# Layer 0 of a four-layer attention and expert stack: routing of the first half placed beside the attention of the other two batches, a constant score row made once, two products merged, loads reordered

## The chip, the cores and the metric

The kernel runs on one NeuronCore of one Trainium2 chip, as a single launch. A core has five engines that run beside each other and are held together by semaphores: PE (TensorE, matrix products; its weight loads are listed apart as PEld), DVE (VectorE), ACT (ScalarE), POOL (GpSimd) and SP (SyncE, which here only issues DMAs and loads registers). Sixteen DMA engines move data between the device memory and the on-chip memory. The metric is the device time of one execution in microseconds (us). Three runs of the kernel before took 1406.45, 1413.10 and 1416.71 us; the median is 1413.1 us.

## What is computed

The input `x` has 4 batches of 512 tokens with 128 features, in float32; `ctx_1024` has 154 rows of 128 features for each batch. Four layers follow each other, and each adds a cross attention and then a mixture of 8 experts to `x`, both of the normalised `x`. This case touches layer 0 alone. Its attention is this (`x` normalised is `encoder_hc`, the context is `decoder_hq`):

```python
w1, w2, w3 = (w_sim[:d], w_sim[d:2 * d], w_sim[2 * d:])
Sim = (encoder_hc @ w1)[:, :, None] + (decoder_hq @ w2)[:, None, :] \
    + jnp.einsum('bid,bjd->bij', encoder_hc * w3, decoder_hq) + b_sim[0]
A = jax.nn.softmax(Sim, axis=2)
hq_hat = jnp.einsum('bij,bjd->bid', A, decoder_hq)
Batt = jax.nn.softmax(jnp.max(Sim, axis=2), axis=1)
hc_bar = jnp.einsum('bi,bid->bd', Batt, encoder_hc)[:, None, :]
hc_hat = jnp.broadcast_to(hc_bar, encoder_hc.shape)
feats = jnp.concatenate([encoder_hc, hq_hat, encoder_hc * hq_hat, encoder_hc * hc_hat], axis=-1)
hcq = feats @ W_qv + b_qv
```

The term `decoder_hq @ w2` is the same for all tokens of a batch. The term `encoder_hc * hc_hat` multiplies each feature by one number of the batch. The expert part of layer 0 takes, for each token, the two experts with the largest of 8 gate values and adds their outputs with softmax weights:

```python
gate_logits = x @ Wg + bg
top_vals, top_idx = jax.lax.top_k(gate_logits, TOP_K)          # TOP_K = 2
h = jnp.einsum('td,edh->eth', xf, W0) + b0[:, None, :]
g = jax.nn.silu(jnp.einsum('td,edh->eth', xf, W1) + b1[:, None, :])
y = jnp.einsum('eth,ehd->etd', h * g, W2) + b2[:, None, :]
```

## The kernel before

**Tiles.** Batch `b` of `x` stays on chip for the whole kernel as `x[b]`, 128 partitions by 4 row tiles (`NI`) by 128 features. The four batches are handled as two halves: half 0 is batches 0 and 1, half 1 is batches 2 and 3.

**Start (L104 to L226).** SP first loads the four batches (L108), then the context in two pieces, `cm` and `ctail` (L112, L113). DVE and POOL make masks and constants. PE transposes the context (L193, L197), and DVE copies it to `ctxT` and to two other arrangements (L194 to L202). L1218 to L1226 load the gate weights and biases of all four layers in nine small DMAs. `layer0_setup` (L956) then loads the score weights `w_sim`, which PE turns into columns (`columns`, L204), the biases and the four 128x128 output matrices `wqv`, and makes two operands: `rhs1` (L964, the context times w3 plus w1) and `w2b` (L966, the column w2 repeated 128 times). L1322 fills two token buffers in device memory, `buf`, with zeros.

**Attention of a batch.** `prepare(b)` normalises `x[b]` (L240), transposes it to `xnT` (L248), and makes the scores of each row tile with two accumulated products, `xnT` by `rhs1` (L975) and `w2b` by `ctxT` (L976). DVE adds the scalar bias while it moves the scores to `sim` (L979), takes row maxima (L987), and ACT makes exponentials with row sums (L992). `tile_of(b)` scales `sim` (L1000), transposes it (L1004, L1009), and multiplies it with the context (L1012, L1013), which gives `hq`. The softmax over the tokens goes through a maximum over partitions (L1016 to L1025), an exponential (L1027), four products with `xn` (L1030) and four with a matrix of ones, which add the exponentials up (L1032). Out of these come three feature tiles `ft` (L1038 to L1040); four products for each of the four row tiles, one per feature block, sum to the output (L1045), which DVE adds to `x[b]` (L1053, L1054).

**Routing of a half.** `route(layer, half)` (L650) is a generator with a `yield` between its stages: statistics of the two batches, which end in a power on POOL (L233); normalising; transposing; gate products (L665); the two largest of eight (`top`, L625); counts and ranks by triangular products (L692, L694); slot numbers `su` (L716) and the expert of each block, `eb` (L744); softmax weights (L769 to L777); and at its end the contribution of the second bias `b2`, which is added to `x` (L792 to L804). At the slot numbers it queues sixteen scatters for POOL in `rows_due` (L733). Each is an indirect DMA (L721) that sends 128 normalised rows to their slots in `buf[half]`. `row_transfers` (L640) issues what is queued.

**Experts of a half.** `experts(layer, half)` (L824) reads `buf[half]` back in groups of four blocks of 128 tokens (`tok`, L838; the load waits for all sixteen scatters), transposes them (L848), and for each of 23 blocks reads the expert number into a register (L856), loads this expert's weights (`w`, L864, three buffers), and does 8 up products (L875), an activation (L890, L891), 4 down products (L902) and a store (L911). Later POOL gathers the outputs (L935), and they are added to `x` (`combine`, L947).

**Order.** `attend_first` (L1257) is the order of layer 0, as written out by hand:

```python
tiles = prepare(0, found[0])
for b in range(B):
    tiles(0)
    if b == 1:
        found.update({k: stats(x[k]) for k in range(2, B)})
    if b == 2:
        beside = Steps(route(layer, 0, *gates[layer]))
    if b < B - 1:
        tiles = prepare(b + 1, found[b + 1])
    if b == 2:
        beside.step(6)
return beside.finish()
```

So `prepare(b + 1)` follows tile `b`, the routing of half 0 is called after the tile of batch 2, and the scatters are issued by the `row_transfers()` at L1331, after the last tile. Then the experts of half 0 begin (L1334), with the routing of half 1 (L1337) between their blocks, its scatters paced two by two behind the blocks' output copies (L910).

Within layer 0 the instructions aren't bound to this order: a scheduler orders each engine's queue at build time by its own estimate, and the written order is one of its inputs. In layers 1 to 3 the attention's order on PE, ACT and DVE is fixed by hand (L1283). [...] Buffers come from pools by tag: two tiles of one tag share its buffers, and a new tile waits until the old one has been read. The tags that matter here are `rows` (two buffers: `w_sim`'s rows, and for layer 1 the wide copies and `wo_r` at L1076), `wv` (one), `aT` (one), `probs` (two), and in PSUM `sc`, `tr` and `av` (two each).

## Time and profile before

| What | us |
|---|---|
| Median of three runs (lowest, highest) | 1413.1 (1406.45, 1416.71) |
| The profiled execution | 1326.58 |
| Its span, first to last instruction | 1324.7 |
| Outside the span | 1.9 |

The profiled execution is 6.1% shorter than the median of the runs. Sums below are made against its own span, and then set beside the median. It had a mean granted TensorE clock of 0.930 of full speed.

The span divides into stages that can be told by which lines run in them. The columns are the stage, its length, PE's busy time, DVE's busy time, and the granted PE clock.

| Stage (us from the start) | Length | PE busy | DVE busy | PE clock |
|---|---|---|---|---|
| Layer 0: start, attention, routing and scatter of half 0 (0 to 118) | 118 | 74.5 | 60.8 | 0.77 |
| Layer 0: experts (118 to 290) | 172 | 151.9 | 92.2 | 0.96 |
| Layer 1: attention (290 to 480) | 190 | 143.8 | 127.8 | 0.89 |
| Layer 1: experts (480 to 600) | 120 | 102.8 | 57.2 | 0.93 |
| Layer 2: attention (600 to 850) | 250 | 233.6 | 158.2 | 0.99 |
| Layer 2: experts (850 to 930) | 80 | 55.0 | 31.2 | 0.89 |
| Layer 3: attention (930 to 1190) | 260 | 242.1 | 159.7 | 0.97 |
| Layer 3: experts (1190 to 1324) | 134 | 95.6 | 61.3 | 0.91 |

How to read it: an engine's busy time is time with an instruction in execution. Matmuls are pipelined, so overlapping ones aren't counted twice, and a busy PE needn't be at its peak. A line such as `L1045 PE MATMUL av<-wqv,ft` names the line in the kernel, the engine, the operation, and the tiles written and read. In a timeline the first number is the start in us from the start of the span, the second the duration of the group, and what stands in brackets is how long the engine had been idle and what ended that. A float32 product appears as two passes, so `x8` is four products.

### The profile page before, as it was taken

To read this page: it belongs to the slowest core of one execution; us is meant where nothing else is said; L and a number is where in the kernel's file an instruction comes from. 1 tells how busy PE (TensorE), PEld (TensorE's weight loads), DVE (VectorE), ACT (ScalarE), POOL (GpSimd) and SP (SyncE) were. 2 spreads that over 40 slices of the span, in tenths; PEclk is the share of its full clock that TensorE was granted. 3 is DMA by queue.
4 is the path that set the end of the run, shared out by engine and by line. 5 is a ranking of instruction groups with operands and counts; after the bars stand their busy time and mean duration, and the time that the engine had idled before them with its cause. 6 is when DMAs were issued, how large, how long until landed. Compare 5 with 4: busy or idle time off the path is not lost.

```text
span 1324.7 us, 26947 instructions
## 1 busy us (share of the span) xinstructions
PE 1099.2 (83%) x9435; PEld 904.1 (68%) x9435; DVE 748.5 (57%) x2057; ACT 588.2 (44%) x2290; POOL 252.4 (19%) x281
## 2 busy tenths in 40 slices
PE   4885897897777778988999999857899999899881
PEld 3774887773343445877787778746778887789781
DVE  5572554656767566433666766424376676646452
ACT  1112443355444444536556655322565665533230
POOL 2023122204000020221000004045030000403424
PEclk8786998998899889989999999988999999999996
DMA  7013575552101121553112223444421211335762
GB/s 220 0 61 98 163 225 179 171 156 80 26 9 37 38 62 50 151 148 93 42 38 46 49 50 102 127 144 140 132 62 34 50 34 33 83 91 163 202 184 57
DMA packets 136996, 126.82 MB, mean 96 GB/s; under 512 B 13466, under 2 KB 116511, under 8 KB 136479
## 3 DMA queue, kind: packets, MB, share of 16 engines
q1 hardware_dynamic: 129695, 110.39, 30.0%
q0 software_dynamic: 7168, 14.69, 3.8%
q8 instruction: 78, 1.28, 0.4%
q14 instruction: 55, 0.45, 0.1%
HBM read 101.31 MB, written 23.72 MB: 94 GB/s over the span
## 4 chain that ended last, share of the span: by engine, by line
PE 38%; DVE 7%; DMA 6%; ACT 3%; issue 3%; POOL 2%; SPq 1%; POOLq 0%; DVEq 0%; ACTq 0%
PE sc L608 5%; PE sc L875 5%; PE tr L368 5%; PE tr L422 4%; PE av L405 4%; PE av L902 4%; DMA w<-in_up 4%; PE sc L593 2%; PE av L387 2%; ACT probs L305 2%; DVE nm L291 2%; POOL yg L935 1%; PE sc L557 1%; PE tr L848 1%; DVE aT L412 1%
## 5 line engine op out<-in xcount | busy, mean ns | idle before, releaser
L305 ACT ACTIVATE probs<-sc,nm 128x154 f32<-128x154 f32 x768 | 286.3, 402 | 169.1 <-DVE nm L291 169.0
L875 PE MATMUL sc<-tokT,w 128*128 128x128 f32 x1528 | 210.8, 287 | 32.8 <-DMA w<-in_up 26.7
L875 PEld LDWEIGHTS sc<-tokT,w 128*128 128x128 f32 x1528 | 189.7, 198 | 46.6 <-DMA w<-in_up 13.0
L291 DVE TENSOR_REDUCE nm<-sc 128x6 f32<-128x924 f32 x144 | 143.2, 1011 | 86.6 <-PE sc L608 50.7
L902 PE MATMUL av<-w,hT 128*128 x1160 | 173.4, 284 | 10.1 <-DVE hT L891 7.3
L305 ACT ACTIVATION_READ_ACCUMULATOR probs<-sc,nm 128x1 f32 x768 | 168.2, 219 | 0.0
L902 PEld LDWEIGHTS av<-w,hT 128*128 128x128 f32 x1160 | 149.9, 195 | 21.2 <-DVE hT L891 11.4
L935 POOL DMA_INDIRECT yg<-ybuf,su x112 | 106.7, 953 | 275.6 <-DVE pT L261 63.7
L233 POOL TENSOR_TENSOR rstd<-ve,nhalf 128x4 f32<-128x4 f32 x32 | 33.2, 1039 | 619.4 <-DVE ve L231 499.2
L721 POOL DMA_INDIRECT buf<-xn,su x112 | 108.1, 965 | 171.3 <-DVE hT L891 43.7
L261 DVE COPY pT<-tr 128x512 f32<-128x512 f32 x160 | 107.4, 688 | 49.2 <-PE tr L368 43.9
L368 PE MATMUL tr<-ident,probs 128*128 128x128 f32 x768 | 121.5, 289 | 0.8 <-DVE rT L334 0.6
L405 PE MATMUL av<-pT,vm 128*64 128x128 f32 (+1 forms) x1536 | 102.7, 284 | 8.8 <-DVE pT L261 8.7
L890 ACT ACTIVATE eg<-sc,w 128x128 f32<-128x128 f32 x184 | 66.2, 367 | 98.5 <-DVE hT L891 72.7
L368 PEld LDWEIGHTS tr<-ident,probs 128*128 128x128 f32 x768 | 86.0, 145 | 28.8 <-issue 12.7
L891 DVE SCALAR_TENSOR_TENSOR hT<-sc,w,eg 128x128 f32<-128x128 f32 x184 | 63.0, 348 | 55.1 <-ACT eg L890 52.7
L910 DVE COPY ys<-av 128x128 f32<-128x128 f32 x168 | 48.5, 289 | 78.7 <-PE av L902 73.3
L405 PEld LDWEIGHTS av<-pT,vm 128*64 128x64 f32 (+1 forms) x1536 | 65.3, 127 | 35.6 <-issue 18.2
L608 PE MATMUL sc<-kT,qT 64*128 64x154 f32 x1024 | 86.5, 308 | 3.5 <-ACT probs L305 3.5
L608 PEld LDWEIGHTS sc<-kT,qT 64*128 64x128 f32 x1024 | 71.0, 189 | 14.3 <-issue 9.7
L593 PE MATMUL sc<-xnT,wq 128*128 128x128 f32 x512 | 67.1, 286 | 2.9 <-ACT probs L305 2.9
L422 PE MATMUL tr<-wo,aT 128*128 128x128 f32 x512 | 66.1, 284 | 1.6 <-DVE xnT L253 1.3
(252 smaller groups left out, 1477.7 us busy)
## 6 DMA issues: line engine op xcount, KB each, us to landing
w<-in_up SPq DMA_DIRECT2D x46, 516.0 KB
w<-in_up SPq DMA_DIRECT2D x76, 258.0 KB
rep<-rd SPq DMA_DIRECT2D x64, 256.0 KB
ybuf<-ys SPq DMA_DIRECT2D x168, 64.0 KB
tok<-buf SPq DMA_DIRECT2D x36, 256.0 KB
w<-in_down SPq DMA_DIRECT2D x3, 2048.0 KB
w<-in_up SPq DMA_DIRECT2D x46, 128.0 KB
buf<-zero SPq DMA_DIRECT2D x2, 1472.0 KB
```

Of the source, the lines that this page charges most:

```text
L261: return nc.vector.tensor_copy(o, i)
L291: nc.vector.tensor_reduce(self.at.heads(self.nm, g, n), self.sc[g][:, :, 0 : n * S2].rearrange("p j (s k) -> p j s k", s=n), AX.X, ALU.max ...
L305: nc.scalar.activation(self.pr[:, h, :], self.sc[g][:, j, s * S2 : (s + 1) * S2], AF.Exp, bias=self.nm[:, h : h + 1], accum_out=self.rs[:, ...
L368: nc.tensor.transpose(q[:, t * P : (t + 1) * P], self.pr[:, h, 0:P], ident)
L405: nc.tensor.matmul(av[rows, cols], v, self.pT[n][:, t, :], start=False, stop=last)
L422: nc.tensor.matmul(o[:, 0:D], self.aT[:, c, :], self.at.wo[:, c, :], start=(c == 0), stop=(c == self.nb - 1))
L593: nc.tensor.matmul(sc[:, c // 4, c % 4 * P : (c % 4 + 1) * P], wq[:, c * P : (c + 1) * P], at.xnT[:, i * P : (i + 1) * P], start=True, sto ...
L608: nc.tensor.matmul(sc[:, j, s * S2 : (s + 1) * S2], at.qT[i][rows, c, :], at.kT[rows, c, :], start=True, stop=True)
L721: ins = nc.gpsimd.indirect_dma_start(out=buf[half], out_offset=bass.IndirectOffsetOnAxis(ap=su[:, t : t + 1], axis=0), in_=xns[t // NI][:, ...
L875: nc.tensor.matmul(dst, w[:, at : at + P], xT, start=True, stop=True)
L902: nc.tensor.matmul(y[:, 0:D], hT[:, fc, :], w2[:, bass.ds(e, 1), fc, :].rearrange("p o d -> p (o d)"), start=(fc == 0), stop=(fc == nf - 1),)
L935: ins = nc.gpsimd.indirect_dma_start(out=yg[:, t, :], out_offset=None, in_=ybuf[half], in_offset=bass.IndirectOffsetOnAxis(ap=su[:, t : t ...
```

## The change

The change touches the loads at the start, `columns`, `layer0_setup` with `prepare` and `tile_of`, `attend_first`, and where the gates are loaded.

- Loads: the first batch of `x`, then `w_sim`, then the context, then the other three batches. The nine gate loads move from ahead of `layer0_setup` to behind it; the statistics of all four batches are asked for ahead of them.
- The constant score row: `row`, two products of `w2b` with the context of two batches each (4 x 154 columns in all) plus the bias, is made once. The scores then need one product for each row tile, and DVE adds `row` where it added the scalar bias.
- Merged products: the number `hc` of each feature is put into the weights, `wc = wqv[3] * hc + wqv[0]`, and the output needs three products for each row tile in place of four. The sum of the exponentials comes from ACT's accumulator (`accum_out=es`), and one product with ones in place of four.
- Order: `prepare(0)`, `prepare(1)`, tile 0, `prepare(2)`, tile 1, then three steps of the routing of half 0, `prepare(3)`, five further steps (up to the slot numbers), the scatters, tile 2, one step, tile 3, the rest.
- Buffers: `w2b` takes tag `rows` in place of `wv`, where `row` now lies; `sim` takes `probs` (two buffers) in place of `aT` (one); `ft` takes `vm`, and `wc` takes `res1`.

```diff
...
 
 
     x_in = a["x"].rearrange("b (i p) d -> b p i d", p=P)
-    x = []
-    for b in range(B):
-        t = xpool.tile([P, NI, D], F32, tag=f"x{b}", name=f"x{b}")
-        nc.sync.dma_start(t, x_in[b])
-        x.append(t)
+    x = [xpool.tile([P, NI, D], F32, tag=f"x{b}", name=f"x{b}") for b in range(B)]
+    nc.sync.dma_start(x[0], x_in[0])
+    sim_rows = p2.tile([3, P], F32, tag="rows", name="sim_rows")
+    nc.sync.dma_start(sim_rows, a["L0_xattn_w_sim"].rearrange("(k p) -> k p", p=P))
     cmt = w1.tile([P, 2, B, D], F32, tag="wo", name="cmt")
     cm, ctail = cmt[:, 0], cmt[0:ST, 1]
     nc.sync.dma_start(cm, a["ctx_1024"][:, 0:P, :].rearrange("b k d -> k b d"))
     nc.sync.dma_start(ctail, a["ctx_1024"][:, P:S2, :].rearrange("b k d -> k b d"))
+    for b in range(1, B):
+        nc.sync.dma_start(x[b], x_in[b])
 
 
     ident = const.tile([P, P], F32, name="ident")
...
         nc.vector.tensor_copy(ct4[:, b], bc(tpv[:, b, :], 1, 4))
     nc.vector.tensor_copy(ct2[:, :, 0 : 2 * ST].rearrange("p b (s k) -> p b s k", s=2), bc(tpv, 2, 2))
 
-    def columns(src, rows, name):
-
-        t = p2.tile([rows, P], F32, tag="rows", name=f"{name}_r")
-        nc.sync.dma_start(t, src)
+    def columns(src, rows, name, t=None):
+
+        if t is None:
+            t = p2.tile([rows, P], F32, tag="rows", name=f"{name}_r")
+            nc.sync.dma_start(t, src)
         q = ps_tr()
         nc.tensor.transpose(q[:, 0:rows], t, ident[:rows, :rows])
         o = const.tile([P, rows], F32, name=name)
...
 
 
     def layer0_setup():
-        wsim = columns(a["L0_xattn_w_sim"].rearrange("(k p) -> k p", p=P), 3, "wsim")
+        wsim = columns(None, 3, "wsim", sim_rows)
         bsim = row_bc(a["L0_xattn_b_sim"], 1, "bsim")
         bqv = row_bc(a["L0_xattn_b_qv"], D, "bqv")
         wqv = w1.tile([P, 4, D], F32, tag="wq", name="wqv")
...
 
         rhs1 = w1.tile([P, B, S2], F32, tag="wk", name="rhs1")
         nc.vector.tensor_scalar(rhs1, ctxT, wsim[:, 2:3], wsim[:, 0:1], ALU.mult, ALU.add)
-        w2b = w1.tile([P, P], F32, tag="wv", name="w2b")
+        w2b = p2.tile([P, P], F32, tag="rows", name="w2b")
         nc.vector.tensor_scalar(w2b, ones, wsim[:, 1:2], None, ALU.mult)
+        row = w1.tile([P, B, S2], F32, tag="wv", name="row")
+        sc = ps_sc()
+        for j in range(2):
+            nc.tensor.matmul(
+                sc[:, j, 0 : 2 * S2],
+                w2b,
+                ctxT[:, 2 * j : 2 * j + 2, :].rearrange("p b k -> p (b k)"),
+                start=True,
+                stop=True,
+            )
+        nc.vector.tensor_scalar(
+            row.rearrange("p (j b) k -> p j (b k)", j=2), sc[:, :, 0 : 2 * S2], bsim, None, ALU.add
+        )
 
         def prepare(b, found):
             xn = norm(x[b], found)
...
             for i in range(NI):
                 s, j = divmod(i, 2)
                 dst = sc[:, j, s * S2 : (s + 1) * S2]
-                nc.tensor.matmul(dst, xnT[:, i * P : (i + 1) * P], rhs1[:, b, :], start=True, stop=False)
-                nc.tensor.matmul(dst, w2b, ctxT[:, b, :], start=False, stop=True)
-            sim = p2.tile([P, NI, S2], F32, tag="aT", name="sim", bufs=1)
+                nc.tensor.matmul(dst, xnT[:, i * P : (i + 1) * P], rhs1[:, b, :], start=True, stop=True)
+            sim = p2.tile([P, NI, S2], F32, tag="probs", name="sim")
             for j in range(2):
-                nc.vector.tensor_scalar(
+                nc.vector.tensor_tensor(
                     sim.rearrange("p (s j) k -> p j s k", j=2)[:, j],
                     sc[:, j, 0 : 2 * S2].rearrange("p (s k) -> p s k", s=2),
-                    bsim,
-                    None,
+                    bc(row[:, b, :], 1, 2),
                     ALU.add,
                 )
             m = small.tile([P, NI], F32, tag="sm", name="sm")
...
             md = small.tile([P, NI], F32, tag="md", name="md")
             nc.vector.tensor_scalar(md, m, mall, None, ALU.subtract)
             ebt = small.tile([P, NI], F32, tag="ebt", name="ebt")
-            nc.scalar.activation(ebt, md, AF.Exp)
+            es = small.tile([P, 1], F32, tag="es", name="es")
+            nc.scalar.activation(ebt, md, AF.Exp, accum_out=es)
             hcp = ps_av()
             for i in range(NI):
                 nc.tensor.matmul(hcp[:, 0:1], xn[:, i, :], ebt[:, i : i + 1], start=(i == 0), stop=(i == NI - 1))
-            for i in range(NI):
-                nc.tensor.matmul(hcp[:, 1:2], ones, ebt[:, i : i + 1], start=(i == 0), stop=(i == NI - 1))
+            nc.tensor.matmul(hcp[:, 1:2], ones, es, start=True, stop=True)
             hd = small.tile([P, 2], F32, tag="hd", name="hd")
             nc.vector.tensor_copy(hd, hcp[:, 0:2])
             hr = small.tile([P, 1], F32, tag="hr", name="hr")
             nc.vector.reciprocal(hr, hd[:, 1:2])
-            ft = p2.tile([P, 3, S], F32, tag="probs", name="ft")
+            hc = small.tile([P, 1], F32, tag="hc", name="hc")
+            nc.vector.tensor_tensor(hc, hd[:, 0:1], hr, ALU.mult)
+
+            wc = p2.tile([P, D], F32, tag="res1", name="wc")
+            nc.vector.scalar_tensor_tensor(wc, wqv[:, 3, :], hc, wqv[:, 0, :], ALU.mult, ALU.add)
+            ft = p2.tile([P, 2, S], F32, tag="vm", name="ft")
             nc.scalar.copy(ft[:, 0, :], hq)
             nc.vector.tensor_tensor(ft[:, 1, :], xnT, ft[:, 0, :], ALU.mult)
-            nc.vector.tensor_scalar(ft[:, 2, :], xnT, hd[:, 0:1], hr, ALU.mult, ALU.mult)
             o = ps_av()
             for i in range(NI):
                 cols = slice(i * P, (i + 1) * P)
-                for k in range(4):
-                    nc.tensor.matmul(
-                        o[:, cols],
-                        xnT[:, cols] if k == 0 else ft[:, k - 1, cols],
-                        wqv[:, k, :],
-                        start=(k == 0),
-                        stop=(k == 3),
-                    )
+                for k, (f, w) in enumerate(((ft[:, 0], wqv[:, 1]), (ft[:, 1], wqv[:, 2]), (xnT, wc))):
+                    nc.tensor.matmul(o[:, cols], f[:, cols], w, start=(k == 0), stop=(k == 2))
             t = p2.tile([P, NI, D], F32, tag="k", name="res")
             nc.vector.tensor_tensor(t, o.rearrange("p (i d) -> p i d", i=NI), bc(bqv, 1, NI), ALU.add)
             nc.vector.tensor_tensor(x[b], x[b], t, ALU.add)
...
     ybuf = [dram.tile([BLK[0] * P, D], F32, name=f"ybuf{h}") for h in range(2)]
     zero = const.tile([P, D], F32, name="zero")
     nc.gpsimd.memset(zero, 0.0)
-    gates = []
...
     setups = (layer0_setup, layer1_setup, layer2_setup, layer3_setup)
 
     class Steps:
...
 
     def attend_first(layer, prepare, found):
 
-        beside = Steps(idle())
-        tiles = prepare(0, found[0])
-        for b in range(B):
-            tiles(0)
-            if b == 1:
-                found.update({k: stats(x[k]) for k in range(2, B)})
-            if b == 2:
-                beside = Steps(route(layer, 0, *gates[layer]))
-            if b < B - 1:
-                tiles = prepare(b + 1, found[b + 1])
-            if b == 2:
-                beside.step(6)
+        tiles = [prepare(b, found[b]) for b in range(2)]
+        tiles[0](0)
+        tiles.append(prepare(2, found[2]))
+        tiles[1](0)
+        beside = Steps(route(layer, 0, *gates[layer])).step(3)
+        tiles.append(prepare(3, found[3]))
+        beside.step(5)
+        row_transfers()
+        tiles[2](0)
+        beside.step(1)
+        tiles[3](0)
         return beside.finish()
 
     ordered = {mybir.EngineType.PE, mybir.EngineType.Activation, mybir.EngineType.DVE}
...
 
     out_v = out.rearrange("b (i p) d -> b p i d", p=P)
     prepare = setups[0]()
+    found = {b: stats(x[b]) for b in range(B)}
+    gates = []
+    for layer, (n, nb) in enumerate((("Wg", "bg"), ("wg", None), ("wg", None), ("W_router", "b_router"))):
+        wg = const.tile([P, E], F32, name=f"wg{layer}")
+        nc.sync.dma_start(wg, a[f"L{layer}_ffn_{n}"])
+        b2 = None
+        if layer != 2:
+            b2 = const.tile([E, D], F32, name=f"b2_{layer}")
+            nc.sync.dma_start(b2, a[f"L{layer}_ffn_b2"])
+        gates.append((wg, row_bc(a[f"L{layer}_ffn_{nb}"], E, f"bg{layer}") if nb else None, b2))
     for half in range(2):
         nc.sync.dma_start(buf[half].rearrange("(p c) d -> p c d", p=P), bc(zero, 1, BLK[0]))
-    found = {b: stats(x[b]) for b in range(2)}
     for layer in range(4):
         w2 = load_down(layer)
         if layer == 0:
```

More of the change, by code (lines that the diff above doesn't have):

```diff
@@ L1217, in tile_xattn_moe_stack @@
     nc.gpsimd.memset(zero, 0.0)
-    gates = []
-    for layer, (n, nb) in enumerate((("Wg", "bg"), ("wg", None), ("wg", None), ("W_router", "b_router"))):
-        wg = const.tile([P, E], F32, name=f"wg{layer}")
-        nc.sync.dma_start(wg, a[f"L{layer}_ffn_{n}"])
-        b2 = None
-        if layer != 2:
-            b2 = const.tile([E, D], F32, name=f"b2_{layer}")
-            nc.sync.dma_start(b2, a[f"L{layer}_ffn_b2"])
-        gates.append((wg, row_bc(a[f"L{layer}_ffn_{nb}"], E, f"bg{layer}") if nb else None, b2))
     setups = (layer0_setup, layer1_setup, layer2_setup, layer3_setup)
```

## The prediction

> **What bounds the kernel now.** The page's slices come first, to find the stage, then its timeline. The chain that ended last is no help: followed back, it breaks off at 544 us, in layer 1.
>
> ```profile
> PE   4885897897777778988999999857899999899881
> PEclk8786998998899889989999999988999999999996
> ```
>
> A slice is 33 us. PE is about half idle in the first, and busy only 8 tenths in the next two with a clock of 7 to 8 tenths. The stretches:
>
> ```profile
> 0.00:15.00 15.00, 3.17 (x14) 2.30 (x15) 11.21 (x65) 1.28 (x1) 8.61 (x29) 1.00 0.58 153
> 15.00:49.00 34.00, 26.01 (x109) 20.66 (x110) 12.57 (x34) 6.00 (x22) 0.00 (x0) 0.70 0.46 148
> 49.00:94.00 45.00, 41.42 (x269) 35.50 (x268) 31.31 (x126) 8.83 (x28) 5.18 (x5) 0.85 0.02 4
> 94.00:118.00 24.00, 3.94 (x24) 3.05 (x22) 5.74 (x25) 0.04 (x1) 14.47 (x15) 0.58 0.37 129
> ```
>
> After the length come busy times of PE, weight loads, DVE, ACT and POOL, then clock, DMA share and GB/s. From 94 to 118 every compute engine but POOL stands still. The timeline says why:
>
> ```profile
> 24.30 1.09 PE L1004 MATMUL tr<-ident,sim 128*128 128x128 f32 x4 [5.01 <-DVE sim L1000]
> 48.02 0.68 DVE L1054 TENSOR_TENSOR x<-x,res 128x512 f32<-128x512 f32 x1
> 64.51 0.69 DVE L1054 TENSOR_TENSOR x<-x,res 128x512 f32<-128x512 f32 x1
> 91.07 0.22 DVE L716 CAST su<-sl 128x8 uint32<-128x8 f32 x2
> 91.52 1.19 POOL L721 DMA_INDIRECT buf<-xn,su  x1 [8.54 <-DVE eb L744]
> 93.48 0.69 DVE L1054 TENSOR_TENSOR x<-x,res 128x512 f32<-128x512 f32 x1
> 110.71 0.95 POOL L721 DMA_INDIRECT buf<-xn,su  x1 [0.30 <-issue]
> 115.98 1.94 PE L848 MATMUL tr<-ident,tok 128*128 128x128 f32 x8 [15.91 <-DMA tok<-buf]
> 117.85 5.67 PE L875 MATMUL sc<-tokT,w 128*128 128x128 f32 x32
> ```
>
> Batches 0 and 1 are final at 48.70 and 65.20, but the slot numbers come at 91.29, because the routing shares the queues with batches 2 and 3. Batch 3 is final at 94.17; then sixteen scatters, 1.26 us apart, run with nothing beside them, and PE waits 15.91 us for the tokens. The first up product at 117.85 is the event to move: afterwards PE is busy 115 of 132 us.
>
> [...] a weight load takes 338 ns at the start and 189 ns later. [...] here scatters land after 2.2, 2.9 or 5.0 us (least, median, most). [...]
>
> **The change, part by part.**
>
> *Loads, gates.* `w_sim` moves up 15 issues, three batches of `x` move behind the context, and nine gate loads (about 0.35 us of SP each) move behind `wqv`. SP's number of issues ahead of the zero fill stays, so fill, down weights and mask land as before; gates are wanted first at about 65, the zeroed buffers at about 74, and the DMA share is 0.02 after 49. But DVE is busy 11.2 of the first 15 us, so an earlier context gains only what leaves DVE's queue ahead of `rhs1`. In the changed program's order that is the second batch's normalising, 1.1 us: operands ready at about 13.7 in place of 14.76. Bounds 0 and 4 us.
>
> *Score row, early batch 1.* At half rate a 154-column pass takes 0.26 us (L975). `row` is 4 passes of 308 columns, 2.1 us; batch 0's score then has 8 passes, 2.1: together 14.2 to 18.4, as long as the sixteen passes before. PE's new order puts batch 1's transposes (1.1) and score (2.1) next, and DVE's puts batch 1's `sim` (0.98, as L979) and maximum (0.79) ahead of batch 0's reciprocal and scaling (1.0). Batch 0's `sim` reaches PE at about 25.0 in place of 24.30: **0.7 lost**.
>
> *Batch 0.* Before, 24.30 to 48.70 is 24.4. Gone from within: batch 1's transposes and score, 1.1 + 3.8; three ones-products, 0.7; 4 of 16 output products, a quarter of 40.87 to 46.37, 1.4. [...] Added: batch 1's four `sim` transposes, 1.1. So 18.4: final at 43.4.
>
> *Batch 1.* Before, 16.5 after batch 0. Gone: half of batch 2's score 1.0, its own transposes 0.6, ones 0.7, output 1.4. Added: DVE now normalises `x[0]` and batch 3 (2.2) ahead of `hd`, of which 0.3 was idle: 1.9. So 14.7: final at 58.1, **7.1 ahead**.
>
> *Routing.* In the new order only batch 3's score and batch 2's scaling stand between. Statistics 1.4, POOL's power 1.05, normalising 1.1, transposes 0.9, copy 0.7, batch 3's score and gate products 2.05, `lg` 0.4, top-two 4.0 (79.30 to 85.5 before, less some 2 of attention), ranks 0.9, then 3.5 as from 87.79 to 91.29: 16.0, where 26.1 lay before. Slot numbers at 74.1, **17.2 ahead**. Bounds 13 and 20.
>
> *Scatters and tail.* They keep their 20.2 us, and from 91.29 to 117.85 is 26.56: first up product at 100.7. Would DVE's work beside slow them? Layer 1's scatters at 484 to 492, beside attention, stand 1.26 apart too: no.
>
> *Cover.* Tiles 2 and 3 now lie beside the scatters. What is left of them on PE after the ranks is 2 x (transposes 1.3, `hq` 2.25, `hcp` 1.2, output 2.7) = 15 us at full rate, 27 at half; from about 71 to 98.8 there are 28, with two register loads of `eb` and two 1.7 us waits for `hd` in it. At full rate hidden; at half some 3 us show. Taken: 0, bound +4. PE's later work behind these tiles is `b2`'s products (2.3) and `wo_r`'s transpose.
>
> *New waits.* (1) On SP the token load is queued behind `wo_r`, whose `rows` buffer now comes free with PE's `Wk` transpose, late in batch 3's tile; if PE is late, tokens are. (2) POOL's powers for half 1 stand behind all scatters (94.5 to 96.6), and on DVE normalising batch 2 waits for them, with batch 3's residual, both `x` additions and the first token copy behind: 1.1 + 0.3 + 3 x 0.7 brings DVE to about 99.2, when the tokens' transposes are due. Taken: 0, bound +1.5. (3) Half 1's routing runs later against the first up product (batch 3 normalised some 4 us after it, not before). Its slots were ready at 141.3, its scatters began at 155.82, paced by L910: 14 us of slack hide that.
>
> *After.* The queues' order in layers 1 to 3 is unchanged; half 0's experts start as a block, so what the start gains stays gained.
>
> Sum: 17.2. Against the profiled execution 1326.6 this gives 1309.4. The runs are 6.5% longer than that execution; if the start is stretched alike, 17.2 is 18.3. I take **1395** from 1413.1, own range 1388 to 1402.
>
> **Rivals.**
>
> *More (1383).* The front is limited by context arrival, [...] and the routing takes 13: 3 to 4 more from loads, 3 from routing, 5 from output products at full rate: 30 in all. [...] Against: DVE's full queue.
>
> *Cover fails (1404).* Tiles 2 and 3 at half rate, or in front of the routing: the wait for tokens becomes one for PE, about 8 of the 17 lost. Shown by no idle time ahead of L848's successor.
>
> *Nothing moves (1412).* The starting point of the experts shifts, but half 1's scatters come late and return it; needs more than 14 us of lateness.
>
> *Slower (1428): clock.* [...] the granted clock falls over the remaining 1200 us, PE-bound for some 1025 (1099.2 less 74.5), then each 0.01 off 0.93 costs 11 us. It decides from 0.016. For it: the same program has taken from 1326 to 1417, more than this edit is worth. Against: [...] POOL, DVE or DMA contention would have to show at 484 to 492, and doesn't.
>
> **How the numbers follow.** Forecast 0.54, more 0.13, cover fails 0.18, nothing 0.04, slower 0.11. A measurement of this kernel can tell about 1%, 14 us, from no change. Faster by that: nine tenths of the forecast (0.49), all of "more", a fifth of "cover fails": 0.65. Slower: 0.10. Within: 0.25. The range leaves out the lower part of "more" and the slower case: 1378 to 1413.
>
> **What would show it.** Right: slot numbers near 74, scatters beside L1012 and L1045 (there as L1025 and L1062), first up product near 100, each later stage of equal length. PE idle ahead of the tokens shrinks from 15.9 to about 8. Wrong: slot numbers past 80; PE without idle time ahead of the tokens; half 1's first token load more than 66 us after the first up product (184.03 less 117.85 before).

## The result, and the profile after

| | Median, us (lowest to highest, runs) | Ratio to before, 95% interval |
|---|---|---|
| Before | 1409.17 (1406.45 to 1416.71, 14) | |
| After | 1403.35 (1396.15 to 1410.25, 14) | 0.9958 (0.994 to 0.9975) |

The change brings 5.8 us (the interval: 3.5 to 8.5) where 18 were forecast. The kernel before has two levels of time, about 1410 us and about 1324 us, which go with the set of runs and not with the kernel: the profile that the prediction read is of the lower level (1326.58), while the timed runs, and the profile after (1400.72, span 1398.8, clock 0.903), are of the upper. So each run below is compared with the kernel before of its own set.

First the page's slices and two stretches of the profile after. A stretch gives its length, then the busy time of PE, weight loads, DVE, ACT and POOL, then the clock, the DMA share and GB/s:

```profile
PE   5679978967777779888999988756889999897881
PEclk8669999987998879999999999878999999899896
```

```profile
84.00:97.00 13.00, 4.77 (x38) 3.92 (x36) 1.45 (x4) 1.16 (x2) 7.58 (x8) 0.72 0.14 45
97.00:108.00 11.00, 10.32 (x59) 9.35 (x60) 8.70 (x37) 1.48 (x2) 1.04 (x1) 0.71 0.25 74
```

A slice is now 35 us; the second and third, which are layer 0 from 35 to 105, have PE at 6 and 7 tenths. From 84 to 97, with two tiles of attention open, PE works 4.8 of 13 us, DVE 1.5, ACT 1.2. The timeline after shows the front (all that comes before the first up product of the experts) and this hole:

```profile
23.20 1.09 PE L1017 MATMUL tr<-ident,sim 128*128 128x128 f32 x4 [2.85 <-DVE sim L1013]
40.62 0.69 DVE L1065 TENSOR_TENSOR x<-x,res 128x512 f32<-128x512 f32 x1
54.70 0.69 DVE L1065 TENSOR_TENSOR x<-x,res 128x512 f32<-128x512 f32 x1
73.12 0.22 DVE L718 CAST su<-sl 128x8 uint32<-128x8 f32 x2
73.58 1.19 POOL L723 DMA_INDIRECT buf<-xn,su  x1 [15.71 <-DVE eb L746]
92.75 0.96 POOL L723 DMA_INDIRECT buf<-xn,su  x1 [0.30 <-issue]
96.25 0.69 DVE L1064 TENSOR_TENSOR res<-av,bqv 128x512 f32<-128x512 f32 x1 [10.31 <-remote]
96.30 0.57 ACT L92 COPY cT<-tr 8x512 f32<-8x512 f32 x1 [11.09 <-remote]
96.99 1.22 PE L1062 MATMUL av<-wqv,ft 128*128 128x128 f32 x4 [8.23 <-DVE res L1064]
98.44 0.34 SPq L1088 DMA_DIRECT2D wo_r<-in_L_xattn_Wo  x1
99.09 0.93 SPq L840 DMA_DIRECT2D tok<-buf  x2
103.98 0.39 PE L1062 MATMUL av<-wc,xnT 128*128 128x128 f32 x2
104.20 0.27 PE L850 MATMUL tr<-ident,tok 128*128 128x128 f32 x1
107.64 3.74 PE L877 MATMUL sc<-tokT,w 128*128 128x128 f32 x32
```

Up to the slot numbers each mark comes as forecast or earlier: batch 0 final at 41.31, batch 1 at 55.39, slot numbers at 73.34 in place of 91.29, the last scatter issued by 93.71 in place of 111.66. Then the lead shrinks. DVE's residual for batch 2 waits 10.31 us and ACT's copy 11.09, with "remote" as releaser, which says that the profile found nothing on the core that let them go. In program order both wait for products of PE whose records end at about 87. PE in turn waits 8.23 for the residual, then does batch 3's tile, and only at 104.20, with no idle time ahead, the first token. The first up product comes at 107.64, not at 100.7. Below, this hole is called the stand-still.

The kernel before, profiled once more at the upper level:

```profile
113.66 5.43 SPq L838 DMA_DIRECT2D tok<-buf  x4
116.75 1.94 PE L848 MATMUL tr<-ident,tok 128*128 128x128 f32 x8 [16.17 <-DMA tok<-buf]
118.63 5.65 PE L875 MATMUL sc<-tokT,w 128*128 128x128 f32 x32
```

There nearly no work lies beside the scatters, and the profile shows no such wait in the front. The front gains 11.0 us (118.63 less 107.64), not 17.2.

### The profile page after: what moved, and what is told of

Read it like the earlier page. It is cut to its first block, busy times and chain, and to the rows that moved or that the text cites. A ratio compares the mean times of both kernels' runs of the same rounds, so it can differ in the third digit from the quotient of the medians.

```text
span 1398.8 us, 26797 instructions
## 1 busy us (share of the span) xinstructions
PE 1128.1 (81%) x9351; PEld 922.8 (66%) x9351; DVE 749.1 (54%) x2062; ACT 588.1 (42%) x2294; POOL 251.7 (18%) x281
## 4 chain that ended last, share of the span: by engine, by line
PE 38%; DVE 8%; ACT 4%; DMA 4%; issue 3%; another core or an unknown queue 2%; POOL 1%; SPq 1%; POOLq 0%; ACTq 0%; DVEq 0%
PE sc L877 5%; PE sc L610 5%; PE av L904 5%; PE av L407 4%; PE tr L370 4%; PE tr L424 4%; DMA w<-in_up 2%; PE sc L595 2%; ACT probs L307 2%; PE av L389 2%; DVE nm L293 2%; PE sc L559 1%; PE tr L850 1%; DVE aT L414 1%
## 5 line engine op out<-in xcount | busy, mean ns | idle before, releaser
L877 PE MATMUL sc<-tokT,w 128*128 128x128 f32 x1528 | 217.4, 292 | 26.5 <-DMA w<-in_up 16.7
L877 PEld LDWEIGHTS sc<-tokT,w 128*128 128x128 f32 x1528 | 196.5, 204 | 39.9 <-issue 10.7
L904 PE MATMUL av<-w,hT 128*128 x1160 | 179.9, 291 | 45.8 <-issue 12.2
L904 PEld LDWEIGHTS av<-w,hT 128*128 128x128 f32 x1160 | 156.0, 201 | 57.4 <-issue 16.9
L912 DVE COPY ys<-av 128x128 f32<-128x128 f32 x168 | 48.4, 288 | 119.0 <-PE av L904 71.2
L595 PE MATMUL sc<-xnT,wq 128*128 128x128 f32 x512 | 70.4, 294 | 2.9 <-ACT probs L307 2.9
L424 PE MATMUL tr<-wo,aT 128*128 128x128 f32 x512 | 69.8, 294 | 2.2 <-DVE xnT L255 1.3
## 6 DMA issues: line engine op xcount, KB each, us to landing
w<-in_up SPq DMA_DIRECT2D x46, 128.0 KB
```

What stands on the lines that cost most here:

```text
L424: nc.tensor.matmul(o[:, 0:D], self.aT[:, c, :], self.at.wo[:, c, :], start=(c == 0), stop=(c == self.nb - 1))
L595: nc.tensor.matmul(sc[:, c // 4, c % 4 * P : (c % 4 + 1) * P], wq[:, c * P : (c + 1) * P], at.xnT[:, i * P : (i + 1) * P], start=True, sto ...
L877: nc.tensor.matmul(dst, w[:, at : at + P], xT, start=True, stop=True)
L904: nc.tensor.matmul(y[:, 0:D], hT[:, fc, :], w2[:, bass.ds(e, 1), fc, :].rearrange("p o d -> p (o d)"), start=(fc == 0), stop=(fc == nf - 1),)
```

## The experiments

**Is the stand-still there again, and in the kernel before?** Both kernels, unchanged:

> The kernel before, unchanged, profiled a second time. Late marks: if the stretches in which PE's results are released 7 to 10 us late (seen in the changed kernel at 86 to 96 us and some twenty times later) are a property of usual executions of either kernel, this profile has about 1405 us, a clock near 0.90, and such stretches from layer 0's experts on, but none before the first up product, which stays at 117 to 119. Caused by the change: the profile has none of them and is near 1325 us, or it has about as much time as 1405 without waits of DVE and ACT for PE of over 5 us.

> The changed kernel, unchanged, profiled a second time. Tied to a place: the stretch from 86 to 96 us in which PE, DVE and ACT stand still beside the scatters is there again, and the first up product comes at 107 to 109. By chance: the stretch is elsewhere or gone, and the first up product comes at 98 to 101 as forecast.

Measured: 1416.56 us and 1400.91. The changed kernel stands still ahead of the same two instructions (8.01 and 8.79 us of waits), and its first up product comes at 109.47. The lists of waits, with the longest in total first (total, times, longest), show the kind in both. Before at the upper level:

```profile
ACT hT L883 <- remote: 30.9, 5, 8.1
DVE aT L412 <- remote: 21.6, 6, 6.4
DVE ys L910 <- remote: 15.5, 3, 8.8
```

After:

```profile
DVE ys L912 <- remote: 32.4, 8, 10.2
ACT hT L885 <- remote: 27.6, 4, 9.5
...
ACT cT L92 <- remote: 11.1, 1, 11.1
DVE res L1064 <- remote: 10.3, 1, 10.3
```

The first profile of before, at 1326.58, has no wait of this kind. They belong to the upper level, in either kernel; the change put work of layer 0 where they strike.

What the level belongs to is open. The record has the chip of each later set: the upper level was seen on chips 13 and 15, the lower on chips 3 (two sets), 6 and 8. No chip showed both, so the level may belong to the chip; no run tests it.

**Which part of the change brings the gain?** old_order is the changed kernel with the order of `attend_first` as it was (the statistics of all batches stay ahead of it); order_only is the kernel before with the new `attend_first`:

```diff
-        tiles = [prepare(b, found[b]) for b in range(2)]
-        tiles[0](0)
...
+        tiles = prepare(0, found[0])
+        for b in range(B):
+            tiles(0)
...
```

This is old_order's edit, shortened. order_only's is the reverse, on the kernel before, with all statistics asked for first, `sim` in two buffers of `probs`, two of the three feature tiles in `vm` and the third in `aT`.

> The changed kernel with the written order of layer 0 as it was (prepare b+1 behind tile b, routing after the tile of batch 2, scatters after batch 3); row, merged products and loads stay changed. If the order brings the gain and the stall eats most of it: the first up product at about 109 to 112 (what the merged products and the row save, 6 to 9 us), nearly no work beside the scatters, so no stall, and a median within 4 us of the changed kernel's 1403. If the stall has nothing to do with the scatters: a stall appears too, and the median is 1407 to 1411.

> The kernel before with the new written order alone (with sim in two buffers of probs, ft in vm and a third feature tile in aT, as two batches are open at once); score products, four output products and loads as before. If the stall belongs to work beside the scatters: it shows again, about 10 us of PE, DVE and ACT standing still within 10 us of the first scatters, first up product at 112 to 116, median 1405 to 1409. If not: first up product at 105 to 108, median 1398 to 1402.

| Run | Level | Median (runs), us | Before | Ratio, 95% interval | First up product |
|---|---|---|---|---|---|
| old_order | upper | 1404.08 (22) | 1412.61 | 0.9947 (0.9928 to 0.9965) | 108.73 |
| order_only | upper | 1412.74 (14) | 1412.61 | 1.0001 (0.9976 to 1.0026) | 115.59 |
| old_order_b | lower | 1310.49 (13) | 1324.1 | 0.9895 (0.9859 to 0.993) | 106.12 |
| order_only_b | lower | 1316.28 (20) | 1322.88 | 0.9952 (0.9926 to 0.9978) | 109.62 |

Without the new order the gain is the same within the intervals; the order alone brings nothing at the upper level, where its forecast was 1405 to 1409. old_order's timeline:

```profile
81.34 0.22 DVE L718 CAST su<-sl 128x8 uint32<-128x8 f32 x2
103.77 5.43 SPq L840 DMA_DIRECT2D tok<-buf  x4
106.86 1.94 PE L850 MATMUL tr<-ident,tok 128*128 128x128 f32 x8 [16.57 <-DMA tok<-buf]
108.73 4.54 PE L877 MATMUL sc<-tokT,w 128*128 128x128 f32 x32
```

Row, merged products and loads alone bring the slot numbers from 91.9 to 81.6, and from there to the first up product it is 27.2 us (26.8 in the kernel before). In the changed kernel the slot numbers come 8.2 earlier still, and the first up product 1.1: the order's part of the lead is lost between them. order_only stands still too, in three pieces, which end at 92.37, 95.96 and 101.71 (1.67, 5.02 and 4.44 us of such waits). Beside order_only_b, the same kernel at the lower level, one sees what that costs: the slot numbers come at 78.6 and 78.7 and the last scatter is issued by 99.4 and 99.2, but the first up product comes 6.0 us later at the upper level.

old_order has no wait of this kind in the front, and yet it gains 8.5 us at the upper level and 13.6 at the lower. The intervals just meet, so this is no proof; but it speaks against the stand-still as the only thing that makes the gain smaller at the upper level. What else could was not found.

**Do the scatters make it?** The scatters of half 0 are left out (`del rows_due[:]` in place of `row_transfers()`, so that these experts read zeros), or held behind batch 3's residual:

```diff
-        row_transfers()
         tiles[2](0)
         beside.step(1)
-        tiles[3](0)
+        row_transfers(behind=tiles[3](0))
```

This is late_scatter's edit; `tile_of` returns its last addition for it.

> The changed kernel without the sixteen scatters of half 0 in layer 0 (that part of the computation is left out: these experts get a buffer of zeros). If the stand-still from 86 to 96 us belongs to the scatters beside it: no engine waits over 3 us for the output product of batch 2; its residual (L1064) comes at about 87 to 88 in place of 96.25, batch 3's at about 96 in place of 104.4, and the first up product at 98 to 101 in place of 107.6. If it belongs to PE's own burst of work or to its instruction stream: the residual stays at 94 to 98, and the first up product at 105 to 109.

> The changed kernel with its scatters held until batch 3's residual is added, so that none lies beside attention; all else stays. If the scatters make the stand-still: none of over 3 us ahead of them, batch 3 final at about 95 to 97, then scatters for 20.2 us and the first up product some 26 us after their start, at about 122 to 124; median about 1416 to 1420. If not: the stand-still shows at 86 to 96 with no scatter beside it, batch 3 final at about 105, first up product at about 131, median about 1426.

> The same kernel as no_scatter (the sixteen scatters of half 0 in layer 0 left out), tried again for a kernel before of about 1410 us. There: if the scatters make the stand-still, the residual of batch 2 comes at 87 to 92 with no wait of over 3 us by DVE or ACT for PE; if PE's own work makes it, the residual comes at 94 to 98 again. Beside a before of about 1324 it repeats 87 to 92 and tells nothing new.

The first set met the lower level (before 1323.58), so no_scatter there (1304.61, first up product 95.50; two repeats at that level gave 1316.51 and 1308.75, with it at 101.10 and 102.98) says nothing on the stand-still. no_scatter_d met the upper one (before 1420.34). Its timeline:

```profile
89.60 0.69 DVE L1064 TENSOR_TENSOR res<-av,bqv 128x512 f32<-128x512 f32 x1 [1.06 <-PE av L1062]
90.04 0.57 ACT L92 COPY cT<-tr 8x512 f32<-8x512 f32 x1 [2.22 <-PE tr L794]
100.51 3.84 PE L877 MATMUL sc<-tokT,w 128*128 128x128 f32 x32
```

The same two instructions wait 1.06 and 2.22 us, and for PE by name; the hole is gone, though the later stages of this profile have such waits as ever (23.5 us at the copy of L912). So at the upper level the stand-still in layer 0 comes and goes with the scatters: it is in two profiles of the changed kernel and one of order_only, and not in this one, which stands alone. Whether they hold PE's results back, and how, stays open. late_scatter, at the lower level, took 1330.41 (ratio 1.0033, 1.0005 to 1.006), first up product at 126.95: with scatters beside nothing behind this order, the kernel is a little slower than before. Its forecast in numbers was for the upper level, which it didn't meet.

**What is lost where nothing stands still?** The changed kernel at the lower level, twice, with the old order beside it:

> The changed kernel, unchanged, beside own_buf and old_order. The kernel before has now shown two levels of time, about 1410 us and about 1324 us. If the stand-still belongs to the upper level: beside a before of about 1324 the changed kernel has no wait of over 3 us beside its scatters, its first up product comes at 100 to 103, and it is 14 to 20 us faster than before; beside a before of about 1410 it is 4 to 10 us faster, as first measured. If the stand-still belongs to the changed order: it shows at either level, and the gain is 4 to 10 us at both.

> The changed kernel, unchanged, as the companion of this call. Stand-still belongs to the level: beside a before of about 1410 the residual of batch 2 waits 8 to 10 us and the first up product comes at 107 to 110; beside a before of about 1324 it waits 1 us and the first up product comes at 103 to 105.

> The same kernel as old_order (row, merged products and loads changed, written order as before). At the upper level it took as long as the changed kernel. If the new order is worth something only where nothing stands still: at the lower level it is 5 to 9 us slower than after_third (first up product at 107 to 109 against 100 to 103). If the order brings nothing at either level: within 3 us of after_third.

> The same kernel as order_only (the kernel before with the new written order and three buffers alone). At the upper level it took as long as the kernel before. If only the stand-still hid the order's worth: at the lower level it is 5 to 9 us faster than before. If the order returns its lead between the scatters and the first expert blocks at either level: within 3 us of before.

after_third took 1311.07 beside 1324.1 (0.9919, 0.9888 to 0.9951), after_fourth 1309.71 beside 1322.88 (0.991, 0.988 to 0.994): 13 us faster. Neither profile's list of waits has a "remote" one; the first up product comes at 104.08 and at 105.94, in both about 1 us later than forecast. The timeline of after_third:

```profile
87.36 0.69 DVE L1064 TENSOR_TENSOR res<-av,bqv 128x512 f32<-128x512 f32 x1 [1.06 <-PE av L1062]
93.21 0.96 POOL L723 DMA_INDIRECT buf<-xn,su  x1 [0.30 <-issue]
95.60 0.94 SPq L840 DMA_DIRECT2D tok<-buf  x2
98.33 0.47 PE L850 MATMUL tr<-ident,tok 128*128 128x128 f32 x1 [4.03 <-DMA tok<-buf]
98.73 2.07 PE L802 MATMUL av<-b,cT 8*128 8x128 f32 x8
100.74 1.75 PE L850 MATMUL tr<-ident,tok 128*128 128x128 f32 x7
103.17 1.12 PE L250 MATMUL tr<-ident,xn 128*128 128x128 f32 x4 [0.68 <-ACT tokT L92]
104.08 5.23 PE L877 MATMUL sc<-tokT,w 128*128 128x128 f32 x32
```

And old_order_b, in which the tiles are done before the scatters end:

```profile
98.97 0.96 POOL L723 DMA_INDIRECT buf<-xn,su  x1 [0.30 <-issue]
106.12 4.57 PE L877 MATMUL sc<-tokT,w 128*128 128x128 f32 x32
```

The tokens come when they should. But PE's queue has the bias products of half 0 (2.07) between the first token's transpose and the rest, and half 1's transposes (1.12) ahead of the up product. From the last scatter's end to the first up product it is 9.9 us in after_third (94.17 to 104.08) and 10.2 in after_fourth; old_order_b needs 6.2 (99.9 to 106.12). Of the 5.6 us by which after_third's slot numbers lead old_order_b's (73.7 against 79.3) 2.0 reach the first up product, of after_fourth's 4.3 only 0.2, and the totals are equal within the intervals. Still, the order alone is worth 6.6 us at this level: its worth and that of the products don't add up.

Two profiles of one kernel at one level lie up to 3.5 us apart at the first up product (own_buf's below), no_scatter's up to 7.5. A difference of 2 us between single profiles shows little.

**Queue of SP, or PE?**

```diff
-        wo_r = p2.tile([P, D], F32, tag="rows", name="wo_r")
+        wo_r = p2.tile([P, D], F32, tag="eg", name="wo_r", bufs=4)
...
-            t = p2.tile([rows, P], F32, tag="rows", name=f"{name}_r")
+            t = p2.tile([rows, P], F32, tag="eg", name=f"{name}_r", bufs=4)
```

> The changed kernel with the rows of Wo, gamma and beta in buffers of their own, so that on SP no load with a wait for PE stands ahead of the token load. If SP's queue made the tokens late: token load at about 94 to 96 in place of 99.09, first up product at 102 to 104, median 1397 to 1400. If PE is what is late (its product for batch 3 ends at 103.98, and the tokens' transposes are queued behind it): the token load moves up by 4 us, the first up product by under 1.5 us, median within 3 us of the changed kernel's 1403.

> The same kernel as own_buf (rows of Wo, gamma and beta in their own buffers), now beside the changed kernel itself. If SP's queue costs time in the changed kernel: 2 to 4 us less than after_third. If PE is what is late: within 2 us of it at the upper level, where PE stands still, and also at the lower, where PE's tile of batch 3 ends just ahead of the tokens.

> The same kernel as own_buf (rows of Wo, gamma and beta in buffers of their own). Beside a before of about 1410 us: if SP's queue adds to what the stand-still costs, token load within 2 us of the last scatter's end in place of 5.4, first up product at 103 to 106 and 4 us or more under the changed kernel's ratio of 0.9958 (a ratio of 0.993 or less); if PE alone is late, first up product at 107 to 110 and a ratio of 0.994 to 0.998. Beside a before of about 1324: ratio 0.986 to 0.989 as in its two other runs, if those were not chance; 0.990 to 0.993, as the changed kernel, if they were.

The tag `eg` has four buffers, which the experts' activations use too; so `wo_r` no longer waits for a buffer of `rows`, but these rows now share with the experts. Three sets, all at the lower level: 1308.5, 1307.14 and 1306.26 us, ratios 0.9869, 0.9873 and 0.9862 (0.9814 to 0.9909 in the last), first up product at 101.94, 104.21 and 100.71. In the set that has both it is 3.9 us under the changed kernel (1307.14 against 1311.07), and its ratio is the lowest of all versions that leave nothing out, three times, but the intervals overlap (own_buf_b 0.9829 to 0.9916, after_third 0.9888 to 0.9951). SP's queue is hardly the reason: the first token load goes out at 95.58, 95.11 and 95.08, and after_third's at 95.60. Another possible reason is that all token transposes now stand behind the bias products, which PE does while it would wait for the tokens anyway (in own_buf_c at 96.68, 1.16 us, the tokens at 98.01). That is not tested by itself, and tokens_first, below, speaks against it as the whole reason. What own_buf does at the upper level wasn't seen.

**PE's order around the tokens.** Both on top of own_buf: tile3_late writes batch 3's tile behind the first two expert blocks, tokens_first does that with the bias products of half 0.

```diff
         first = Steps(experts(layer, 0, routed[0], w2)).step(2)
+        if layer == 0:
+            rest.pop()(0)
```

In tile3_late `rest` holds batch 3's tile, as here; in tokens_first it holds the bias products, called without the 0.

> As the run with buffers of their own, and the tile of batch 3 written behind the first two expert blocks, so that PE has only batch 2's rest and the bias products between the slot numbers and the tokens. If the cover that fails is PE's work beside the scatters: PE waits for tokens again, the first up product comes at 100 to 103, and the median falls to 1394 to 1399 as long as half 1's routing still lies within its slack. If the stand-still itself holds the tokens (loads or scatters land late): first up product at 106 to 109, median 1401 to 1406.

> As own_buf (rows of Wo, gamma and beta in buffers of their own), and the bias products of half 0 (L802) written behind the first two expert blocks. Before a lower level of 1324: if PE's order around the tokens costs the 3.7 us by which the changed kernel falls behind between last scatter and first up product (9.9 us against 6.2), first up product at 100 to 102, 6 to 7 us behind the last scatter, and a median 2 to 4 us under the changed kernel's. If what the tokens wait for is only the weights or the half clock: first up product at 103 to 105, median within 1.5 us. Before an upper level of 1410: 3 to 5 us under the changed kernel if PE's order counts, none if the stand-still sets all.

tile3_late: 1316.52 (0.996, 0.9937 to 0.9983), 8.0 us behind own_buf in its set, though the first up product at 101.55 is as early; half 1's routing waits for batch 3, now final at 128.0, and its scatters start at 149.0, not 138.6 as own_buf's. What the start gains, half 1 seems to return. tokens_first: 1311.74 (0.9907, 0.9883 to 0.9932), where 2 to 4 us under the changed kernel were forecast and after_fourth took 1309.71. Its timeline:

```profile
98.32 1.97 PE L858 MATMUL tr<-ident,tok 128*128 128x128 f32 x8 [4.42 <-DMA tok<-buf]
100.22 5.58 PE L885 MATMUL sc<-tokT,w 128*128 128x128 f32 x32
```

In both, the first up product comes 6.2 us behind the last scatter's end, as in old_order_b; with own_buf alone it is 7.1 to 10.5, in the changed kernel 9.9 and 10.2. So at this level the delay is work in PE's queue ahead of the tokens, and it goes when either piece of it moves behind. tokens_first's is 3.9 us earlier than after_third's, and the kernel is no faster. Its eighth block starts at 132.70, after_third's at 132.88, after_fourth's at 133.07, old_order_b's at 133.35: leads of up to 6 us at the first up product are gone by the eighth block. In that stretch of tokens_first PE works nearly all the time (32.57 us of the 35 from 100 to 135), the bias products lie in it, and the granted clock is 0.61 from 100 to 105 and 0.66 from 110 to 115 (1.00 from 105 to 110). The other case is on record too: own_buf_c's eighth block starts at 128.16, so there 4.7 us of the lead over after_third are still there; its first two blocks took 3.74 us, those of tokens_first 5.58:

```profile
98.01 0.66 PE L850 MATMUL tr<-ident,tok 128*128 128x128 f32 x4 [0.18 <-DMA tok<-buf]
100.71 3.74 PE L877 MATMUL sc<-tokT,w 128*128 128x128 f32 x32
```

## Why the prediction was wrong

- **Start, batches 0 and 1, routing:** right, with errors that cancel. Operands at 12.9 (forecast 13.7), batch 0's `sim` at PE at 23.20 (25.0, "0.7 lost"; it was 1.1 won), batch 0 final 41.31 (43.4), batch 1 55.39 (58.1); the routing took 17.95 in place of 16.0; slot numbers 73.34 (74.1). That the slot numbers fit is in part luck. The 18.4 us for batch 0 hold a price for `wc` that no trace of before showed; in the profile after `hc` took 0.16 us (L1051) and `wc` 0.35 (L1054), where L1040 took 0.55.
- **Scatters:** 20.1 us, as forecast. But "Would DVE's work beside slow them?" asked only half of the question. The other half is whether the work beside them is slowed. At the upper level it waited up to 11.09 us beside them, and 2.22 us in no_scatter_d; the profile that was read, of the lower level, shows no such wait.
- **Cover: this is the step that failed** ("Taken: 0, bound +4"). From the last scatter's end to the first up product the kernel before and old_order need 6.4 us at the upper level; the changed kernel takes 13.9 (107.64 less 93.71) and 13.4 in its second profile. So the two tiles beside the scatters cost 7.5 and 7.0, not 0. At the lower level they cost 3.7 and 4.0 (9.9 and 10.2 against 6.2), by PE's order, as tile3_late and tokens_first show: `b2`'s products were named as lying behind the tiles, and priced at nothing. The difference of 3 to 4 us goes with the stand-still, and no_scatter_d shows that the stand-still goes with the scatters. Half the clock, which the bound was made for (in the profile that was read the granted clock was 0.50 from 24 to 36 us and from 85 to 90, and 1.00 from 70 to 80), didn't open the hole, in which PE stood idle for 8.23 us; it shows in what came behind (four passes of L1062 take 1.06 us at 102.33, at a granted clock of 0.50, and 0.61 at 103.53, at 1.00). PE's wait for the tokens, forecast at about 8 us, was 4.03 and 0.44 at the lower level, and none at the upper.
- **What the Cover step doesn't explain:** the slot numbers lead by 18.5 us at the upper level (91.86 less 73.34), the first up product by 11.0 (9.2 in the second profile), and the medians by 5.8. The last part, some 3 to 5 us, stays open. The profiled executions don't show where it goes: the spans of before_again and after are 15.6 apart, and single runs of the kernel before in that set range over 20 us (1401.09 to 1421.02).
- **New waits:** (1) came true: the token load went out 0.65 behind `wo_r` (98.44, 99.09), which PE's stand-still held; at the lower level `wo_r` is at 89.85 and costs nothing there. (2) is in the traces (DVE normalises at 95.27, residual at 96.50 in after_third), hidden behind the tokens. (3) held: half 1's first token load is 65.9 us after the first up product (173.55 less 107.64), against 66 as the sign of being wrong.
- **After ("what the start gains stays gained"):** for the whole change nearly so at the lower level: 13.8 and 11.9 us at the first up product (117.85 less 104.08 and 105.94) and 13 in the medians. At the upper level 11.0 and 9.2 become 5.8. Within the change it doesn't hold: tokens_first's 5.9 us of lead over old_order_b don't reach the end.
- **The rivals.** "Cover fails (1404)" has the number (1403.35) and the sign, PE without idle time ahead of the tokens, but by another mechanism than it names; that the number fits is luck. "Nothing moves" fell: half 1's scatters start at 142.21, 14.3 us ahead of the kernel before's at this level. "More" fell with the routing, which took 17.95 and not 13. "Slower: clock" asked for a fall of 0.016, and that didn't come. But a smaller one did: at the lower level the mean clock of the runs was 0.929 and 0.930 in the changed kernel beside 0.937 in the kernel before, at the upper 0.902 in old_order beside 0.907. By the prediction's own 11 us for each 0.01 that would be worth 5 to 9 us, no less than what is missing at the lower level (17.2 less 13). Whether it is a cause no run tells; late_scatter, in which PE waits longest for the tokens (24.76 us), has the lowest clock of its level (0.924), so a longer wait of PE didn't go with a higher clock there.
- **The scale.** To take 17.2 us from one execution and stretch it by 1.065 was the wrong way to carry it to runs 6.5% longer. That excess is no even stretch: the last store of layer 0's experts comes at 295.3 in the one profile of the kernel before and at 295.5 in the other, so all of it lies behind, in part as waits beside indirect DMAs; and the change moved work of layer 0 into such a place. At the lower level the changed kernel's medians, 1311.07 and 1309.71, lie near the 1309.4 of the sum. This too is luck in part: the profile that was read is 2.5 and 3.7 us above the kernel before's medians in these sets (1324.1 and 1322.88), and the gain there is 13 and not 17.2.
- **Slips of the working that cost nothing:** `w_sim` moves up 14 issues, not 15, and DVE doesn't stand still from 94 to 118; it works 5.74 of the 24 us.

## What to carry to other kernels

Before a sum made in one profiled execution is carried to runs that take longer, find out where the longer ones lose their time: overlap bought at such a place can be worth less than in the profile. When two parts of a change both shorten the same chain, undo each alone; here the plain savings (row, products, loads) did all of it that the runs can tell, and the rewritten order, worth 6.6 us alone at best, nothing on top. When work is moved beside a wait, list everything that then stands in the queue ahead of the next step, and price each piece. A first event that moves up is a milestone and not a gain until a later one, some blocks on, has moved too.

## What the runs showed of the hardware

At the upper level DVE, ACT and PE's weight loads have waits of up to 11.09 us whose releaser the profile doesn't find. The profile after has 23 of them, and each ends within 3.7 us after the issue of an indirect DMA from POOL: beside the gathers at 297 to 326 and the scatters at 484 to 495 and 1272 to 1294, among others. The lists of waits of the other five profiles of that level show 15 to 25 each. In layer 0 they come and go with the sixteen scatters (11.09 us in the profile after, 2.22 in no_scatter_d). At the lower level the first profile of before has none; no wait of this kind stands in the lists of after_third, after_fourth, own_buf_c and old_order_b, nor in the timelines of the other nine from 85 to 101 us. That they lie together is shown, how the one makes the other isn't. What makes a set of runs fall on one level or the other wasn't found.

The first two blocks' 32 up passes took 3.74 us in own_buf_c, where PE had waited 0.18 and 0.24 us ahead of its token transposes, and 5.97 in own_buf, after a wait of 4.02. The length of the wait alone doesn't set it: old_order took 4.54 after 16.57.
